# Cross-attention and a mixture of experts on one core: loads to 128 partitions, statistics in one piece, and results fetched earlier

## The chip, the core and the metric

The kernel runs on one core of a Trainium2 chip. The metric is device microseconds for one launch. Three runs of the kernel before gave 607.83, 608.56 and 609.25 us; the median is 608.56. Everything is float32.

## What is computed

```python
def _L0_xattn_ref(query, kv, Wq, Wg, bg, Wkv, Wo):      # 16 heads of 32
    q = query @ Wq.T
    gate = jax.nn.sigmoid(query @ Wg.T + bg)
    k, v = jnp.split(kv @ Wkv.T, 2, axis=-1)
    # heads split; feature map: x + 1 for x > 0, else exp(x)
    kv_summary = jnp.einsum('bhsd,bhse->bhde', k, v)
    k_sum = k.sum(axis=-2)
    z = 1.0 / (jnp.einsum('bhld,bhd->bhl', q, k_sum)[..., None] + EPS)
    attn = jnp.einsum('bhld,bhde->bhle', q, kv_summary) * z
    return attn * gate @ Wo.T                            # heads joined

def _L0_ffn_ref(x, Wr, We, be):                          # 8 experts, 2 a token
    w, sel = jax.lax.top_k(jnp.einsum('bsd,de->bse', x, Wr), 2)
    gate = softmax(w) spread over the chosen experts
    for e in range(8):
        out = out + gate[..., e:e+1] * (x @ We[e] + be[e])

x = x + _L0_xattn_ref(_layernorm(x), ctx_2048, ...)      # x: 4 x 512 x 512, ctx: 4 x 1024 x 512
x = x + _L0_ffn_ref(_layernorm(x), ...)
```

## The kernel before

The kernel goes through the four batches in turn. For each batch there are two parts. `kv_tiles` takes eight tiles of 128 context rows: each one is loaded by SyncE (`load_ctx`, three buffers), multiplied by the key and value halves of wkv (matmuls `pk` and `pv`), the keys go through the feature map (L250 to L252, VectorE and ScalarE), and the sums of keys times values gather in PSUM (`kvs`). Then come the queries (`pq`), the gates (`pg`, sigmoid with bias at L423), the products with the sums (`pz`, `pn`) and the output projection (`po`). The first four context tiles of the next batch are worked off between products and output, the other four behind it, so that TensorE always has something to do.

The layer norm of the attention's input is taken in a layout of its own. `load_blocks` brings x into SBUF in pieces that need only a 32x32 transpose on VectorE (`normalized_T`, L297 and L301). The mean and deviation of each row are computed from an ordinary copy of x (`layernorm_stats`). They must then get to other partitions, and that goes through memory: `spread_moments` writes means and reciprocal deviations to `moments` in two DMAs on GpSimd's queue (L281), waits, and reads them back in four (L286). `load_rows` (wg and wq) and a loop of the same form for the expert weights (L382 and L383) load weights in the matching order of rows, in four DMAs of 32 partitions each, where each partition gets four pieces of 2 KB. For wg the columns are then turned by seven copies on GpSimd (L169). The seven gate biases are loaded by SyncE between the seven pieces of wo (L949 and L950).

After a batch's attention, `choose` normalizes its rows, computes the router's logits, and picks two experts a token. `dispatch` computes a place for every choice and scatters the rows, with GpSimd's indirect DMAs, into `stream`, a region of memory for each expert that has been set empty before (`set_empty`). Then `run` works off tiles of 128 rows of the stream: 17 early ones, mixed in with the fourth batch, and up to 22 late ones, of which 18 (`SURE`) are a fixed loop. For a tile SyncE loads the rows in four DMAs of 32 partitions (L765, tile `xg`, five buffers in all), and the last two columns in a fifth (tile `of`). VectorE transposes (L782), TensorE multiplies by the expert's weights (`pe`), VectorE adds the bias (L814), and GpSimd scatters the results to `result` (L818). In the loop, `rows(j + 5)`, `expert(j)` and `turned(j + 3)` are one step.

The two results of every token are then fetched back (L889), weighed and added to x (L902), and stored (L913), for sixteen tiles of 128 tokens. For the first fourteen this is spread over the steps of the late loop by a table of steps, `begins`: the fetch at that step, the addition three steps later, the store after one more. `queue_of` gives the queue: GpSimd's up to step 12, ScalarE's from step 13 on. A fetch waits for as many puts as `READ` names; whether that was enough is computed in the kernel, and tiles for which it was not are read again at the end. The last two tiles follow after the loop. The work on each engine's queue stands in an order that is mostly fixed in the program (`keep_in_program_order`, `issue_after`); what is left free is placed by the scheduler of the framework.

Of the kernel before, what the change touches and what calls it, by code (L numbers as in the profile page):

```python
# [9 lines left out]
F32 = mybir.dt.float32  # L10
# [7 lines left out]
P = 128  # L18
B, L, S, D = 4, 512, 1024, 512
E, F = 8, 512  # L20
HD = 32
# [32 lines left out]
def xattn_moe_kernel(  # L54
# [32 lines left out]
    result = dram.tile([NOWHERE + 2 * L, F], F32, name="result")  # L87


    moments = dram.tile([B, HD, NT, P // HD, 2], F32, name="moments")  # L90


    def matmul(**operands):
# [8 lines left out]
    def load(dst, src):  # L102
        latest["load"] = nc.sync.dma_start(out=dst, in_=src)  # L103
        tc.keep_in_program_order(latest["load"])
# [27 lines left out]
    def load_rows(dst, w):  # L132


        for i in range(NC):
            load(dst[ts(i, HD)], w.rearrange("(c f) i n -> i f c n", f=HD)[i])

    wkv_sb = wpool.tile([P, NC, 2 * D], F32, tag="wkv", name="wkv_sb")
    wq_sb = wpool.tile([P, NC, D], F32, tag="wq", name="wq_sb")
# [3 lines left out]
    nc.gpsimd.memset(wr_sb, 0.0)  # L143
    bg_sb = wpool.tile([P, NC], F32, name="bg_sb")
    we_sb = wpool.tile([P, E, NC, F], F32, name="we_sb")
    we_rows = we.rearrange("e (c f) i n -> e i f c n", f=HD)

    ctx_tiles = {}

# [104 lines left out]
    def layernorm_stats(tiles):  # L254
        mv = small.tile([P, NT, 2], F32, tag="mv", name="mv")
        for t in range(NT):
            st = small.tile([P, 6], F32, tag="st", name="st")
            nc.vector.bn_stats(st, tiles[t])
            nc.vector.bn_aggr(mv[:, t, :], st)
        rstd = small.tile([P, NT], F32, tag="rstd", name="rstd")  # L260
        nc.scalar.activation(rstd, mv[:, :, 1], AF.Sqrt, bias=eps_sb)
        nc.vector.reciprocal(rstd, rstd)
        return mv, rstd

    def normalize(dst, xt, t, mv, rstd):
        nc.vector.tensor_scalar(
            dst, xt, mv[:, t, 0:1], rstd[:, t : t + 1], ALU.subtract, ALU.mult
        )

    def transposed(dst, src):  # L270

# [4 lines left out]

    def spread_moments(b, tiles):

        mv, rstd = layernorm_stats(tiles)
        for k, of in enumerate((mv[:, :, 0], rstd)):  # L280
            nc.gpsimd.dma_start(  # L281
                out=moments[b, :, :, :, k].rearrange("t n j -> j t n"), in_=of
            )
        ln = small.tile([P, NT, P // HD, 2], F32, tag="ln", name="ln", bufs=1)
        for i in range(NC):
            nc.gpsimd.dma_start(  # L286
                out=ln[ts(i, HD)].rearrange("t n j k -> t (n j k)"),
                in_=moments[b].rearrange("t n j k -> t (n j k)"),
            )
        return ln  # L290

    def normalized_T(xT, t, blocks, ln):

        rows = blocks[:, ts(t, D)].rearrange("p (j f) -> p j f", f=P)
        with tc.issue_after(latest["map"].ins):
            for j in range(P // HD):
                nc.vector.tensor_scalar(  # L297
                    rows[:, j], rows[:, j], ln[:, t, j, 0:1], ln[:, t, j, 1:2],
                    ALU.subtract, ALU.mult,
                )  # L300
            nc.vector.transpose(  # L301
                xT[:, :, ts(t, P)].rearrange("p c (j t) -> p j c t", t=HD),
                rows.rearrange("p j (c f) -> p j c f", f=HD),
            )
# [41 lines left out]
    def kv_blocks(psum):  # L346
        for h in range(P // HD):
            r = slice(h * HD, (h + 1) * HD)
            nc.scalar.copy(h_kv[r], psum[r, :, r])
            nc.vector.tensor_copy(h_ks[r, :, h : h + 1], psum[r, :, P : P + 1])  # L350
# [23 lines left out]
    def kv_tiles(b, lo, hi, between=None, inside=None):  # L374
        for s in range(lo, hi):
            nxt = (b, s + 2) if s + 2 < NS else (b + 1, s + 2 - NS)
            if nxt[0] < B and nxt not in loaded_ctx:
                loaded_ctx.add(nxt)
                ctx_tiles[nxt] = load_ctx(*nxt)
            if b in (1, 2) and s % 2 == 0:  # L380
                e = (b - 1) * E // 2 + s // 2
                for i in range(NC):  # L382
                    load(we_sb[ts(i, HD), e], we_rows[e, i])  # L383
            for e in (s,) if b else (2 * (s - NS // 2), 2 * (s - NS // 2) + 1):
                if e >= 0:
                    set_empty(b, e)
            if s == 0:
                sums[b] = pkv.tile([P, NC, 2 * P], F32, tag="kvs", name="kvs")
            k = made.pop(s) if s in made else keys(b, s)
            if (b, s) == (0, 0):  # L390
                made[1] = keys(0, 1)
            if inside is not None and s == lo:
                inside()
            v = values(b, s)
            if s > 0:
                kv_add(sums[b], s - 1, *pending[b])
            pending[b] = k, v
            if between is not None:
                between(s - lo)
        if hi == NS:  # L400
            kv_add(sums[b], NS - 1, *pending[b])
# [121 lines left out]

    routed = {}

    def choose(b, mv, rstd):

        rows = []
        batch = work.tile([P, NT, ROW], F32, tag="row", name="rows", bufs=1)
        for t in range(NT):  # L530
            row = batch[:, t, :]
            normalize(row[:, 0:D], xs[b][t], t, mv, rstd)
            nc.gpsimd.tensor_copy(row[:, D : D + 1], home[:, b * NT + t : b * NT + t + 1])
            rows.append(row)

        xT = big.tile([P, NC, L], F32, tag="aT", name="x2T")
        for t in range(NT):
            transposed(xT[:, :, ts(t, P)], rows[t])
            yield

        ps = pmm.tile([P, L], F32, tag="mm", name="ps")
        for c in range(NC):
            matmul(
                out=ps[ts(c, HD), :],
                lhsT=wr_sb[:, c, :],
                rhs=xT[:, c, :],
                start=True,
                stop=True,
                tile_position=(0, c * HD),
            )  # L550
        share = work.tile([P, L], F32, tag="z", name="share")
        nc.scalar.copy(share, ps)
        yield
        pl = pmm.tile([P, NT, E], F32, tag="mm", name="pl")
        for t in range(NT):
            matmul(
                out=pl[:, t, :], lhsT=share[:, ts(t, P)], rhs=by_expert, start=True, stop=True
            )
        lg = small.tile([P, NT, E], F32, tag="lg", name="lg")
        nc.vector.tensor_copy(lg, pl)  # L560

        def largest(name):
            m = small.tile([P, NT, 1], F32, tag=f"m{name}", name=f"m{name}")
            hot = small.tile([P, NT, E], F32, tag=f"hot{name}", name=f"hot{name}")
            at = small.tile([P, NT, 1], F32, tag=f"at{name}", name=f"at{name}")
            nc.vector.tensor_reduce(m, lg, AX.X, ALU.max)
            nc.vector.tensor_tensor(hot, lg, m.to_broadcast([P, NT, E]), ALU.is_equal)
            nc.vector.tensor_tensor(hot, hot, rank, ALU.mult)
            nc.vector.tensor_reduce(at, hot, AX.X, ALU.max)
            nc.vector.tensor_tensor(hot, hot, at.to_broadcast([P, NT, E]), ALU.is_equal)  # L570
            return m, hot, at

        m1, hot1, first = largest("1")
        nc.vector.scalar_tensor_tensor(lg, hot1, -BIG, lg, ALU.mult, ALU.add)
        m2, hot2, _ = largest("2")

        routed[b] = rows, m1, hot1, first, m2, hot2
        yield
# [159 lines left out]
    def run(lists, lo, n, early):  # L738
# [3 lines left out]
        def rows(j):  # L742
# [10 lines left out]
            of = small.tile([P, 2], F32, tag="of", name="of", bufs=8)  # L753
            rows_of = stream[ds(row, P), :]
            parts = []
            for i in range(NC):
                parts.append(
                    (
                        xg[ts(i, HD), 0:D].rearrange("t (j f) -> t j f", j=NC),
                        rows_of[:, ts(i, P)].rearrange("(j t) f -> t j f", t=HD),  # L760
                    )
                )
            parts.append((of, rows_of[:, D:ROW]))
# [162 lines left out]
    def plan(step, *what):  # L926
        at_step.setdefault(min(step, SURE), []).append(what)

    def queue_of(step):
        return nc.gpsimd if step < SURE - 5 else nc.scalar  # L930

    begins = (-3, -2, -1, 0, 5, 6, 7, 8, 10, 11, 14, 15, SURE - 2, SURE - 2)
    for g, (lo, hi, most) in enumerate(READ):
        for t in range(lo, hi):
            plan(begins[t], fetch, t, most, queue_of(begins[t]), g)
    for t, begin in enumerate(begins):
        step = begin + (3 if begin < SURE - 4 else SURE)
        plan(step, add, t, gates if step < SURE else gates_end)
        plan(step + 1, store, t, queue_of(step + 1))

    def also(j):
        for what, *of in at_step.pop(j, []):
# [3 lines left out]
    xT = new_xT()  # L946
    kv_tiles(0, 0, 3)
    for g, a, b, n in turned:
        load(bg_sb[b : b + n, g : g + 1], bg[a : a + n, g : g + 1])  # L949
        load(wo_sb[b : b + n, g, :], wo[a : a + n, g, :])  # L950
    ln = spread_moments(0, xs[0])

# [2 lines left out]
            normalized_T(xT, t, blocks, ln)  # L955

    kv_tiles(0, 3, NS, between)
    kv_blocks(sums[0])
    for b in range(B):
        more = b + 1 < B  # L960
# [60 lines left out]
            for _ in range(3):  # L1021
                next(early)
        attention_out(b, aT)
        choice = choose(b, *layernorm_stats(xs[b]))
        if more:

            def between(i):
# [133 lines left out]
```

## Time and profile before

| What | us |
|---|---|
| Median of three runs | 608.56 |
| The profiled execution's own time | 610.59 |
| Span of the profile | 608.9 |
| TensorE busy | 576.7 |
| VectorE busy | 289.6 |
| Loads of late and early rows (xg), 140 issues of | 64 KB |
| Loads of expert weights (we), 32 issues of | 256 KB |

The profile is one execution, and its span is shorter than the execution's own time by 1.7 us that lie around it. A `pk` or `pv` of one tile is eight passes on TensorE (four matmuls, two passes each) and takes 3.43 us without a gap. The chain of work that ended last is followed back from the last instruction, at each step to what released it. "DMA xg<-stream" in it stands for the time between the issue of that transfer and its landing. In tables by stage each row is a stretch of the span.

### The profile page before, as it was taken

The page shows a single profiled execution, that of the slowest core. Times are in us where ns is not written, and L with a number is a line of the kernel's source. Part 1 is how long each engine was busy: PE and PEld are TensorE (multiplying, and loading weights), DVE is VectorE, ACT ScalarE, POOL GpSimd, SP SyncE. Part 2 cuts the span into 40 slices and gives each one's busy share as a digit, 9 for nine tenths or more (in the row PEclk, how much of TensorE's full clock was granted, in tenths as well). Part 3 has the DMA queues.
Part 4 walks back from the last instruction along what each step waited for, and adds up shares of the span by engine and source line. Part 5 has one row for each costly group of instructions (what it writes and reads, how often), then busy time and mean ns, then how long its engine had stood idle before and what let it go on. Part 6 is the DMA issues. An engine that isn't in the chain of part 4 may idle for free.

```text
span 608.9 us, 6440 instructions
## 1 busy us (share of the span) xinstructions
PE 576.7 (95%) x1780; PEld 270.0 (44%) x1780; DVE 289.6 (48%) x732; ACT 109.3 (18%) x168; POOL 120.5 (20%) x289
## 2 busy tenths in 40 slices
PE   7989999999999999999999999999999999998950
PEld 3545544454555435445543454554344443443420
DVE  2215254354317443541564355128765579473863
ACT  1311241220313321122242121221300110000000
POOL 4230021000001510000061100003211237444630
PEclk9989999999999999999999999999999999999995
DMA  8979995374490698627338660952255444889866
GB/s 283 166 122 355 340 197 48 116 238 131 121 277 19 140 240 261 190 87 209 103 140 147 236 203 5 315 221 108 89 119 121 121 122 167 251 235 295 243 225 212
DMA packets 78933, 109.87 MB, mean 180 GB/s; under 512 B 13229, under 2 KB 39853, under 8 KB 78768
## 3 DMA queue, kind: packets, MB, share of 16 engines
q1 hardware_dynamic: 68112, 79.91, 49.0%
q0 software_dynamic: 8336, 24.29, 12.2%
q10 hardware_dynamic: 2448, 5.24, 2.6%
q8 instruction: 15, 0.25, 0.2%
q14 instruction: 22, 0.18, 0.1%
HBM read 50.19 MB, written 59.96 MB: 181 GB/s over the span
## 4 chain that ended last, share of the span: by engine, by line
PE 74%; DMA 9%; DVE 6%; SPq 4%; issue 4%; POOL 1%; DVEq 0%; ACTq 0%; POOLq 0%
PE pk L94 18%; PE pv L94 16%; PE pq L94 9%; PE po L94 9%; PE pg L94 7%; PE pe L94 5%; PE kvs L94 4%; DMA xg<-stream 4%; DMA cT<-in_cT_dram 3%; SPq L765 2%; SPq L103 1%; PE pn L94 1%; PE pt L97 1%; DMA result<-y,to 1%; DMA of<-stream 1%
## 5 line engine op out<-in xcount | busy, mean ns | idle before, releaser
L94 PE MATMUL pk<-wkv_sb,cT 128*128 128x512 f32 x256 | 119.4, 611 | 6.4 <-DMA cT<-in_cT_dram 6.4
L94 PE MATMUL pv<-wkv_sb,cT 128*128 128x512 f32 x256 | 115.2, 593 | 0.0
L250 DVE TENSOR_SCALAR ex<-pk 128x512 f32<-128x512 f32 x32 | 22.1, 692 | 135.1 <-PE pk L94 135.1
L94 PEld LDWEIGHTS pv<-wkv_sb,cT 128*128 128x128 f32 x256 | 48.4, 190 | 62.3 <-issue 59.8
L94 PEld LDWEIGHTS pk<-wkv_sb,cT 128*128 128x128 f32 x256 | 48.0, 196 | 60.9 <-issue 53.4
L94 PE MATMUL pe<-we_sb,xgT 128*128 x144 | 62.8, 594 | 3.9 <-DVE xgT L782 3.9
L94 PE MATMUL pe<-we_sb,turned_rows 128*128 x136 | 60.4, 596 | 1.9 <-DVE turned_rows L782 1.5
L94 PE MATMUL pg<-xT,wg_sb 128*128 128x512 f32 x128 | 56.7, 595 | 0.0
L94 PE MATMUL pq<-xT,wq_sb 128*128 128x512 f32 x128 | 56.6, 596 | 0.0
L94 PE MATMUL po<-wo_sb,aT 128*128 128x512 f32 x128 | 55.6, 592 | 0.0
L818 POOL DMA_INDIRECT result<-y,to x35 | 36.4, 1041 | 94.0 <-DVE y L814 91.3
L251 ACT ACTIVATE ex<-ex 128x512 f32<-128x512 f32 x48 | 30.2, 629 | 137.5 <-DVE ex L250 117.3
L330 POOL MEMSET v<- 128x4 f32 x32 | 3.3, 108 | 245.4 <-PE kvs L94 245.3
L94 PEld LDWEIGHTS pe<-we_sb,xgT 128*128 128x128 f32 x144 | 27.1, 190 | 39.4 <-issue 32.2
L624 POOL DMA_INDIRECT stream<-rows,slot x32 | 32.9, 1027 | 51.7 <-DVE acc L587 22.2
L94 PEld LDWEIGHTS kvs<-v,k 128*128 128x128 f32 x256 | 33.3, 191 | 16.0 <-issue 14.2
L94 PEld LDWEIGHTS pe<-we_sb,turned_rows 128*128 128x128 f32 x136 | 25.2, 190 | 34.0 <-issue 29.9
L94 PEld LDWEIGHTS pg<-xT,wg_sb 128*128 128x128 f32 x128 | 24.0, 190 | 32.1 <-issue 32.1
L94 PEld LDWEIGHTS po<-wo_sb,aT 128*128 128x128 f32 x128 | 24.1, 190 | 29.2 <-issue 28.7
L94 PEld LDWEIGHTS pq<-xT,wq_sb 128*128 128x128 f32 x128 | 23.8, 190 | 27.3 <-issue 27.3
L94 PE MATMUL kvs<-v,k 128*128 128x129 f32 x256 | 34.1, 275 | 0.0
L252 DVE SCALAR_TENSOR_TENSOR k<-pk,ex 128x512 f32<-128x512 f32 x32 | 22.1, 691 | 21.6 <-ACT ex L251 21.6
(183 smaller groups left out, 459.7 us busy)
## 6 DMA issues: line engine op xcount, KB each, us to landing
stream<-empty SPq DMA_DIRECT2D x24, 1028.0 KB
stream<-empty SPq DMA_DIRECT2D x8, 1285.0 KB
xg<-stream SPq DMA_DIRECT2D x140, 64.0 KB
we_sb<-in_we_dram SPq DMA_DIRECT2D x32, 256.0 KB
cT<-in_cT_dram SPq DMA_DIRECT2D x31, 256.0 KB
y<-result POOLq DMA_DIRECT2D x10, 512.0 KB
x<-in_x_dram SPq DMA_DIRECT2D x16, 256.0 KB
blocks<-in_x_dram SPq DMA_DIRECT2D x16, 256.0 KB
```

The costliest lines, as they stand in the source:

```text
L94: tc.keep_in_program_order(nc.tensor.matmul(**operands))
L97: tc.keep_in_program_order(nc.tensor.transpose(dst, src, ident))
L103: latest["load"] = nc.sync.dma_start(out=dst, in_=src)
L250: nc.vector.tensor_scalar(ex, src, 0.0, None, ALU.min)
L251: nc.scalar.activation(ex, ex, AF.Exp)
L252: latest["map"] = nc.vector.scalar_tensor_tensor(dst, src, 0.0, ex, ALU.max, ALU.add)
L330: nc.gpsimd.memset(v[:, :, P : P + 1], 1.0)
L624: put = nc.gpsimd.indirect_dma_start(out=stream, out_offset=bass.IndirectOffsetOnAxis(ap=slots[i][:, t, :], axis=0), in_=rows[t], in_offse ...
L765: load = nc.sync.dma_start(out=dst, in_=src)
L818: put = nc.gpsimd.indirect_dma_start(out=result, out_offset=bass.IndirectOffsetOnAxis(ap=home_i, axis=0), in_=y, in_offset=None, bounds_ch ...
```

## The change

It does four things.

1. The loads of wg, wq, the expert weights and the experts' rows are cut the other way: still four DMAs each, but each now goes to all 128 partitions, with one piece a partition (2 KB for weights, 512 bytes for rows). What was four groups of 32 partitions is now an outermost dimension of 4 on the side of the source. The blocks of x (`load_blocks`) are loaded as before.
2. The reciprocal deviations are written beside the means into `mv`, and one DMA a batch brings both to `moments`, eight numbers (32 bytes) a partition; `normalize` and `normalized_T` read them there. In the order of instructions the writes of the moments come behind the seven copies of wg on GpSimd for the first batch. For the second and third batch's end the next statistics, with ScalarE's square root, stand ahead of the router's copy `share`, where they stood behind it.
3. The seven loads of gate biases leave SyncE's queue for GpSimd's.
4. In `begins`, the tiles 4 to 9 are fetched one step earlier and the tiles 10 and 11 two steps earlier. GpSimd's queue now serves the steps up to 11. The stores of the tiles 8 and 9 go to SyncE's queue, later ones to ScalarE's as before.

```diff
-    moments = dram.tile([B, HD, NT, P // HD, 2], F32, name="moments")
+    moments = dram.tile([B, HD, P // HD, NT, 2], F32, name="moments")
...
-        for i in range(NC):
-            load(dst[ts(i, HD)], w.rearrange("(c f) i n -> i f c n", f=HD)[i])
+        for c in range(NC):
+            load(dst[:, c, :], w[ts(c, HD)].rearrange("f i n -> i f n"))
...
-        rstd = small.tile([P, NT], F32, tag="rstd", name="rstd")
-        nc.scalar.activation(rstd, mv[:, :, 1], AF.Sqrt, bias=eps_sb)
-        nc.vector.reciprocal(rstd, rstd)
-        return mv, rstd
+        dev = small.tile([P, NT], F32, tag="rstd", name="dev")
+        nc.scalar.activation(dev, mv[:, :, 1], AF.Sqrt, bias=eps_sb)
+        nc.vector.reciprocal(mv[:, :, 1], dev)
+        return mv
...
-        mv, rstd = layernorm_stats(tiles)
-        for k, of in enumerate((mv[:, :, 0], rstd)):
-            nc.gpsimd.dma_start(
-                out=moments[b, :, :, :, k].rearrange("t n j -> j t n"), in_=of
-            )
-        ln = small.tile([P, NT, P // HD, 2], F32, tag="ln", name="ln", bufs=1)
+        mv = layernorm_stats(tiles)
+        nc.gpsimd.dma_start(out=moments[b].rearrange("t j n k -> j t (n k)"), in_=mv)
+        ln = small.tile([P, P // HD, NT, 2], F32, tag="ln", name="ln", bufs=1)
...
-                for i in range(NC):
-                    load(we_sb[ts(i, HD), e], we_rows[e, i])
+                load_rows(we_sb[:, e], we[e])
...
-            for i in range(NC):
+            for j in range(P // HD):
                 parts.append(
                     (
-                        xg[ts(i, HD), 0:D].rearrange("t (j f) -> t j f", j=NC),
-                        rows_of[:, ts(i, P)].rearrange("(j t) f -> t j f", t=HD),
+                        xg[:, ts(j, P)],
+                        rows_of[ts(j, HD), 0:D].rearrange("t (i f) -> i t f", i=NC),
                     )
                 )
...
-    def queue_of(step):
-        return nc.gpsimd if step < SURE - 5 else nc.scalar
-
-    begins = (-3, -2, -1, 0, 5, 6, 7, 8, 10, 11, 14, 15, SURE - 2, SURE - 2)
+    def queue_of(step, behind=nc.scalar):
+        return nc.gpsimd if step < SURE - 6 else behind
+
+    begins = (-3, -2, -1, 0, 4, 5, 6, 7, 9, 10, 12, 13, SURE - 2, SURE - 2)
...
-        plan(step + 1, store, t, queue_of(step + 1))
+        plan(step + 1, store, t, queue_of(step + 1, nc.sync if step < SURE - 4 else nc.scalar))
...
-        load(bg_sb[b : b + n, g : g + 1], bg[a : a + n, g : g + 1])
         load(wo_sb[b : b + n, g, :], wo[a : a + n, g, :])
...
     kv_tiles(0, 3, NS, between)
+    for g, a, b, n in turned:
+        nc.gpsimd.dma_start(out=bg_sb[b : b + n, g : g + 1], in_=bg[a : a + n, g : g + 1])
     kv_blocks(sums[0])
```

More of the change, by code (lines that the diff above doesn't have):

```diff
@@ L145, in xattn_moe_kernel @@
     we_sb = wpool.tile([P, E, NC, F], F32, name="we_sb")
-    we_rows = we.rearrange("e (c f) i n -> e i f c n", f=HD)
     ctx_tiles = {}
@@ L259, in layernorm_stats, with normalize @@
             nc.vector.bn_aggr(mv[:, t, :], st)
-        rstd = small.tile([P, NT], F32, tag="rstd", name="rstd")
-        nc.scalar.activation(rstd, mv[:, :, 1], AF.Sqrt, bias=eps_sb)
-        nc.vector.reciprocal(rstd, rstd)
-        return mv, rstd
-    def normalize(dst, xt, t, mv, rstd):
-        nc.vector.tensor_scalar(
-            dst, xt, mv[:, t, 0:1], rstd[:, t : t + 1], ALU.subtract, ALU.mult
-        )
+        dev = small.tile([P, NT], F32, tag="rstd", name="dev")
+        nc.scalar.activation(dev, mv[:, :, 1], AF.Sqrt, bias=eps_sb)
+        nc.vector.reciprocal(mv[:, :, 1], dev)
+        return mv
+    def normalize(dst, xt, mv):
+        nc.vector.tensor_scalar(dst, xt, mv[:, 0:1], mv[:, 1:2], ALU.subtract, ALU.mult)
     def transposed(dst, src):
@@ L277, in spread_moments @@
     def spread_moments(b, tiles):
-        mv, rstd = layernorm_stats(tiles)
-        for k, of in enumerate((mv[:, :, 0], rstd)):
-            nc.gpsimd.dma_start(
-                out=moments[b, :, :, :, k].rearrange("t n j -> j t n"), in_=of
-            )
-        ln = small.tile([P, NT, P // HD, 2], F32, tag="ln", name="ln", bufs=1)
+        mv = layernorm_stats(tiles)
+        nc.gpsimd.dma_start(out=moments[b].rearrange("t j n k -> j t (n k)"), in_=mv)
+        ln = small.tile([P, P // HD, NT, 2], F32, tag="ln", name="ln", bufs=1)
         for i in range(NC):
             nc.gpsimd.dma_start(
-                out=ln[ts(i, HD)].rearrange("t n j k -> t (n j k)"),
-                in_=moments[b].rearrange("t n j k -> t (n j k)"),
+                out=ln[ts(i, HD)].rearrange("t j n k -> t (j n k)"),
+                in_=moments[b].rearrange("t j n k -> t (j n k)"),
             )
@@ L297, in normalized_T @@
                 nc.vector.tensor_scalar(
-                    rows[:, j], rows[:, j], ln[:, t, j, 0:1], ln[:, t, j, 1:2],
+                    rows[:, j], rows[:, j], ln[:, j, t, 0:1], ln[:, j, t, 1:2],
                     ALU.subtract, ALU.mult,
@@ L524, in xattn_moe_kernel, with choose @@
     routed = {}
-    def choose(b, mv, rstd):
+    def choose(b, mv):
         rows = []
@@ L531, in choose @@
             row = batch[:, t, :]
-            normalize(row[:, 0:D], xs[b][t], t, mv, rstd)
+            normalize(row[:, 0:D], xs[b][t], mv[:, t])
             nc.gpsimd.tensor_copy(row[:, D : D + 1], home[:, b * NT + t : b * NT + t + 1])
@@ L1023, in xattn_moe_kernel @@
         attention_out(b, aT)
-        choice = choose(b, *layernorm_stats(xs[b]))
+        choice = choose(b, layernorm_stats(xs[b]))
         if more:
```

## The prediction

> **What bounds the kernel now.** I read the page's busy shares first, then the chain that ended last, then TensorE's own timeline of the last hundred microseconds, then a table of the DMA load by stage.
>
> ```profile
> span 608.9 us, 6440 instructions
> PE 576.7 (95%) x1780; PEld 270.0 (44%) x1780; DVE 289.6 (48%) x732; ACT 109.3 (18%) x168; POOL 120.5 (20%) x289
> ...
> q1 hardware_dynamic: 68112, 79.91, 49.0%
> ```
>
> TensorE is the bound nearly everywhere: 576.7 of 608.9 us. So the change can win only at places where TensorE waits, some 32 us in all, but it can lose without such a limit. The chain shows where those places are: the start and the end.
>
> ```profile
> 26.61 12.30 DMA cT<-in_cT_dram
> 39.05 5.37 PE pk L94 x8
> 44.42 3.43 PE pv L94 x8
> ...
> 590.47 5.94 DMA result<-y,to
> 596.95 5.62 DMA y<-result
> ```
>
> The context tile asked for at 26.61 lands at 38.91; TensorE idles 1.99 us before 39.05, and its next eight matmuls take 5.37 instead of 3.43 us. That stall is worth 2.0 + 1.9 = 3.9 us. The last two lines are the tail: the last result's way to memory and back. Between them, 50 to 440 us, the chain is TensorE without a gap. In the late loop of experts TensorE stands nearly gapless too, at 3.43 us a tile:
>
> ```profile
> 522.53 7.03 PE L94 MATMUL pe<-we_sb,xgT 128*128 x16
> 530.13 31.17 PE L94 MATMUL pe<-we_sb,xgT 128*128 x72 [0.58 <-DVE xgT L782]
> 562.91 20.87 PE L94 MATMUL pe<-we_sb,xgT 128*128 x48 [1.60 <-DVE xgT L782]
> 585.47 3.70 PE L94 MATMUL pe<-we_sb,xgT 128*128 x8 [1.70 <-DVE xgT L782]
> ```
>
> The three gaps (3.9 us) are late rows (xg). Now the DMA load, by stage; the columns are busy time of PE, PEld, DVE, ACT and POOL, then clock, mean busy share of the 16 DMA engines, and GB/s:
>
> ```profile
> 4.00:14.00 10.00, 9.55 (x17) 4.14 (x18) 1.78 (x6) 0.76 (x2) 4.19 (x34) 1.00 1.04 353
> 14.00:24.00 10.00, 10.00 (x31) 4.93 (x30) 4.10 (x11) 3.38 (x5) 3.38 (x3) 1.00 1.04 221
> 24.00:36.00 12.00, 12.00 (x35) 5.79 (x34) 2.77 (x4) 3.13 (x4) 0.00 (x0) 1.00 1.19 105
> 462.00:474.00 12.00, 12.00 (x29) 5.32 (x28) 5.10 (x12) 0.30 (x1) 0.00 (x0) 1.00 0.45 89
> 514.00:532.00 18.00, 15.95 (x38) 6.91 (x38) 9.30 (x19) 0.00 (x0) 8.22 (x18) 1.00 0.80 239
> 532.00:550.00 18.00, 18.00 (x44) 7.95 (x43) 13.23 (x24) 0.00 (x0) 8.83 (x24) 1.00 0.83 238
> 550.00:568.00 18.00, 16.39 (x39) 7.12 (x38) 8.72 (x17) 0.00 (x0) 7.43 (x18) 1.00 0.90 259
> 568.00:590.00 22.00, 19.48 (x45) 8.09 (x43) 14.08 (x26) 0.00 (x0) 10.85 (x24) 1.00 0.78 263
> ```
>
> Loads to 128 partitions (4 to 14 us) move 353 GB/s; the loads of wg and wq, each to 32 partitions (14 to 24), only 221 at the same busy share. From 24 to 36 us, with the 4-byte writes of the moments under way, the full engines move 105. And in the late loop (514 to 590) the engines are already 78 to 90% busy. That is the cover that matters: TensorE is one step ahead of a DMA bound.
>
> **The change, part by part.**
>
> *Wide loads (wg, wq, we, xg).* They seem to answer the second row: 353 instead of 221 GB/s. But the source of each new load is a pattern of 4 x 32 x n, with the 4 outermost, against 128 partitions of destination; before, both sides had 32 outermost. [...] What the trace has: the loads issued by SyncE in the issue table add up to 62720 data packets from 337 issues; the 68112 of queue q1 are 5392 more, which is 337 x 16. So each issue closes with 16 small packets, one for each engine, and all of them have an outermost 32 or more on both sides. No issue of SyncE here has a 4 outermost. [...]
>
> The price. By the first row an engine moves 353/16 = 22 GB/s; the packet records give 84 ns for 2048 bytes, or 24. Four engines: 88 to 98 GB/s, so 1 MB takes 10.7 to 11.9 us.
>
> *Start.* The four engines are free of earlier loads at 14 us (first row's end). Then wg 10.7 to 11.9, one tile 0.7, wq 10.7 to 11.9, the blocks 4.7 (1 MB at 221) and the tile that TensorE waits for 0.7: 41.5 to 43.9, landing 1.5 later: 43 to 45.4 instead of 38.9. **+5** (0 to +8).
>
> *Middle.* The expert weights (we) are 256 KB issues in fours: 10.7 us on four engines per two steps of 7.76 us, beside 2 x 2.8 for emptying the stream and 2 x 0.7 for tiles: 17.7 in 15.5 us. The tiles are asked for two steps (15.5 us) ahead, and the stretch is followed by 13.7 us of attention output, so by itself this hides. If that cover failed, it would cost 2.2 us per pair of steps, in eight pairs. What may not hide: on ScalarE, in the order of instructions, the square root of the next batch's statistics now stands ahead of the copy `share` in two batches. That copy ran at 183.03, with the matmul that needs it at 184.05. Now it waits for x, whose loads queue behind we. Price: from nothing to 4 us each; the statistics of the last x tile, 0.69 + 0.17, and the root, 0.30, alone use the 1.0 us of slack, and x comes some 2 us late. **+4** (0 to +8) for both.
>
> *Experts.* A tile of rows is 512 packets of 512 bytes. The records' median is 27 ns; the row of 462 to 474, where nearly nothing else runs, gives 0.45 x 16 x 12 us for four tiles, 42 ns each, with the 32-partition crowding in it. On four engines: 512 x 27/4 = 3.5 us a tile, up to 5.4. I take 3.5, since crowding should go. Early tiles: the first lands 2.5 us later (3.5 instead of about 1), before TensorE has others to do. **+2.5** (0 to +5). Late loop: 18 tiles x 3.5 = 63 us on these four. Also on them is a sixteenth each of the rest: 514 to 576 moves 239 x 18 + 238 x 18 + 259 x 18 + 263 x 8 = 15.4 MB, less 4.7 MB of rows = 10.7 MB, at 353 to 410 GB/s 26 to 30 us. Together 90 us from the first late request (514.6), so the last rows land at about 607 instead of 578: +29 to +33; **+32** (low +12 if half of the others' work moves behind the rows; at 5.4 us a tile +65).
>
> *Statistics in one piece.* Two writes of 512 4-byte pieces a batch (1.74 and 1.53 us of GpSimd at 18 and 20 us) become one of 128 pieces of 32 bytes. 24 to 36 us moved 1.26 MB that takes 5.7 us at 221 GB/s: some 6 us of DMA time come free. If the four engines were not the late ones, the tile would land before it is needed and the 3.9 us stall would go. With them it is not what ends last: **0** (−3.9 to 0). The new wait of the moments behind the seven copies of wg on GpSimd is covered: ln is needed at 46.5.
>
> *Gate biases.* Seven issues leave SyncE (0.34 to 1.35 us each, 4.3 together, from 27 to 43 us) for GpSimd, idle from 8.6 to 18. The next tile, issued at 43.79, was not waited for: **0** (−1 to 0).
>
> *Results sooner, late stores elsewhere.* Eight fetches of 512 KB come one or two steps earlier; each waits in GpSimd's queue for the put of the step before, with the next put behind it (2 us of cover by five y buffers). Two stores of 0.59 us leave GpSimd for SyncE, whose last row request is by then out. The work of the four engines ahead of the last rows stays the same: **−1** (−4 to +3).
>
> Sum: 5 + 4 + 2.5 + 32 − 1 = +42.5. The profiled execution's own time is 610.59 (span 608.9), the median 608.56, 2 us lower, as the whole; 608.6 + 42 = 650.6, say **650**.
>
> **Rivals.**
> *Sixteen engines.* The hardware cuts the 128 partitions in 16, or takes the four engines in turn. [...] Then the second row becomes the first, the start's 3.9 us and some 3 us of the late gaps go, the tail gains 1: 608.6 − 8 = 601. It decides at about 7 engines: 512 x 27/k + 30/18 stays under 3.43 us a tile from k = 8.
> *Four engines, but mostly hidden.* The rows overtake the results and fetches, which then drain on the twelve idle engines; start and middle keep their cover by the 6 us of freed DMA time. Late +12, elsewhere +3: 624. Against it: the results share those four engines too, and each needs all of its parts.
> *No effect.* Gains and losses cancel; nothing in the rows singles this out.
>
> **Numbers.** Four engines, late loop bound: 0.68 (632 to 682). Mostly hidden: 0.14 (612 to 632). Sixteen engines: 0.16 (596 to 606). No change: 0.02. A measurement of this kernel tells about 0.2% from nothing. The range 612 to 682 leaves out the sixteen-engine case and little else. Slower 0.82, same 0.02, faster 0.16.
>
> **What would show it.** Right: q1 has fewer packets by 12 for each new load (180 of them); 14 to 36 us below 221 GB/s; the first big wait for a tile ends after 42; in the late loop TensorE waits for xg on most tiles at 5 to 6 us each, DMA share near half. Wrong: the packets stay 16 an issue and 14 to 24 us moves over 300 GB/s; or the loop keeps 3.5 us a tile.

## The result and the profile after

The changed kernel takes 674.36 us (median of four runs, 672.74 to 678.69), the kernel before in the same session 608.9 us (607.83 to 609.35). The ratio is 1.109, with a 95% interval of 1.1035 to 1.1143: slower by 65 us. The profiled execution took 674.17 us, its span is 672.5.

First the page's busy shares and the line of SyncE's DMA queue (packets, MB, share of the engines):

```profile
span 672.5 us, 6434 instructions
PE 595.0 (88%) x1780; PEld 275.7 (41%) x1780; DVE 291.9 (43%) x732; ACT 108.9 (16%) x168; POOL 113.2 (17%) x292
...
q1 hardware_dynamic: 65616, 80.42, 37.9%
```

Two things are to be seen. TensorE is busy for 18.3 us more, with the same 1780 matmuls. And q1 has 2496 packets fewer. That number comes out exactly: the seven bias loads that left take 624 with them (512 of data and 7 x 16 that close them), two stores of 256 KB that came in bring 288, and 180 loads that close with 4 packets instead of 16 lose 180 x 12 = 2160. 68112 − 624 + 288 − 2160 = 65616. That is what is left if every one of the changed loads ran on four engines. The packets that close a load have 4 bytes in the packet records: q1 has 5904 of that size before, 512 of them biases, and 3152 after. The packets under way agree: from 14 to 24 us the kernel before has 16 or 17 packets of 2 KB under way for 71% of the time; from 26 to 35 us the kernel after has four of them for 78% and five for 20%, and never more than six. All four loads of wq had been asked for by 25.52, so they share these four; which of the sixteen engines they are, the records don't name.

The table by stage of the kernel after (busy time of PE, PEld, DVE, ACT and POOL, then clock, DMA share, GB/s):

```profile
14.00:24.00 10.00, 10.00 (x30) 4.88 (x29) 3.85 (x11) 3.38 (x5) 0.00 (x0) 1.00 0.33 113
24.00:36.00 12.00, 12.00 (x37) 5.89 (x36) 2.77 (x4) 3.13 (x4) 3.80 (x10) 1.00 0.43 118
36.00:46.00 10.00, 0.81 (x8) 0.61 (x6) 0.00 (x0) 0.59 (x1) 1.81 (x5) 0.66 0.83 152
...
590.00:620.00 30.00, 21.45 (x44) 8.42 (x43) 12.04 (x23) 0.00 (x0) 10.55 (x29) 0.89 0.59 189
```

From 14 to 36 us a share of 0.33 to 0.43 of the DMA engines is busy, though SyncE has a full list of loads to give out: 113 and 118 GB/s. From 36 to 46 us TensorE does next to nothing. In the late loop the DMA share is 0.59 where it was 0.78 to 0.90, and TensorE works 21.45 of 30 us, at a clock of 0.89.

TensorE's own timeline of the kernel after shows three of the four places where the time went (start, length; in brackets the idle time before and what ended it). They are the start, the middle (one of two such waits) and the late loop:

```profile
48.54 5.84 PE L94 MATMUL pk<-wkv_sb,cT 128*128 128x512 f32 x8 [11.73 <-DMA cT<-in_cT_dram]
54.22 3.60 PE L94 MATMUL pv<-wkv_sb,cT 128*128 128x512 f32 x8
...
198.62 1.87 PE L94 MATMUL pl<-by_expert,share 128*128 128x8 f32 x8 [4.68 <-ACT share L545]
...
563.49 8.83 PE L94 MATMUL pe<-we_sb,xgT 128*128 x16 [2.58 <-DVE xgT L775]
...
578.50 3.70 PE L94 MATMUL pe<-we_sb,xgT 128*128 x8 [1.46 <-DVE xgT L775]
...
605.68 8.91 PE L94 MATMUL pe<-we_sb,xgT 128*128 x16 [5.62 <-DVE xgT L775]
...
632.60 12.54 PE L94 MATMUL pe<-we_sb,xgT 128*128 x24 [5.80 <-DVE xgT L775]
```

The second column matters as much as the brackets. Before, eight passes take 3.60 to 3.70 us from the first start to the last end, and 16 take 7.03. Sixteen passes behind a gap of 2.58 or 5.62 us take 8.8 to 8.9 us; eight passes behind a gap of 1.46 us take the usual 3.70. So these two gaps cost their own length and some 1.8 us more, and the one of 1.46 us its length alone.

The ledger, by positions in the two timelines:

| Stage | Mark in the timeline, before and after | Longer by, us | Predicted |
|---|---|---|---|
| Start | `pv` of the context tile that is waited for, 44.26 and 54.22 | 10.0 | 5 |
| Middle | first `pq` of the last batch, 409.66 and 435.64 | 16.0 | 4 |
| Early experts | first late `pe`, 522.53 and 557.21 | 8.7 | 2.5 |
| Late loop | end of the last `pe`, 589.17 and 651.32 | 27.5 | 32 |
| Tail | end of the span, 608.9 and 672.5 | 1.4 | −1 |

### The profile page after: what moved, and what is told of

Its sections match the earlier page's. It is cut to its first block, busy times and chain, and to the rows that moved or that the text cites. A ratio compares the mean times of both kernels' runs of the same rounds, so it can differ in the third digit from the quotient of the medians.

```text
span 672.5 us, 6434 instructions
## 1 busy us (share of the span) xinstructions
PE 595.0 (88%) x1780; PEld 275.7 (41%) x1780; DVE 291.9 (43%) x732; ACT 108.9 (16%) x168; POOL 113.2 (17%) x292
## 3 DMA queue, kind: packets, MB, share of 16 engines
q10 hardware_dynamic: 2160, 4.72, 2.2%
## 5 line engine op out<-in xcount | busy, mean ns | idle before, releaser
L94 PE MATMUL pe<-we_sb,xgT 128*128 x144 | 71.0, 644 | 23.1 <-DVE xgT L775 22.9
L94 PE MATMUL pe<-we_sb,turned_rows 128*128 x136 | 63.9, 623 | 7.1 <-DVE aT L465 3.9
L94 PE MATMUL pq<-xT,wq_sb 128*128 128x512 f32 x128 | 60.7, 631 | 0.0
L94 PEld LDWEIGHTS pq<-xT,wq_sb 128*128 128x128 f32 x128 | 25.5, 204 | 29.8 <-issue 29.5
L775 DVE STREAM_TRANSPOSE xgT<-xg 128x512 f32<-128x512 f32 x18 | 12.8, 712 | 53.9 <-DMA xg<-stream 53.9
```

The costliest lines, as they stand in the source:

```text
L94: tc.keep_in_program_order(nc.tensor.matmul(**operands))
L775: latest["turn"] = nc.vector.transpose(xT.rearrange("p c (j t) -> p j c t", t=HD), xg[:, 0:D].rearrange("p (j c f) -> p j c f", j=NC, f=HD),)
```

## The experiments

My theory: the wide loads run on four engines, and are the whole loss, by three separate ways (rows, expert weights, wg and wq). The rivals: one of the other parts loses too (the square root ahead of `share`, SyncE's longer issues, the earlier fetches), or 128 partitions are bad in themselves.

### All loads back in their old form (e1)

From the kernel after:

```diff
-        for c in range(NC):
-            load(dst[:, c, :], w[ts(c, HD)].rearrange("f i n -> i f n"))
+        for i in range(NC):
+            load(dst[ts(i, HD)], w.rearrange("(c f) i n -> i f c n", f=HD)[i])
...
-                        xg[:, ts(j, P)],
-                        rows_of[ts(j, HD), 0:D].rearrange("t (i f) -> i t f", i=NC),
+                        xg[ts(i, HD), 0:D].rearrange("t (j f) -> t j f", j=NC),
+                        rows_of[:, ts(i, P)].rearrange("(j t) f -> t j f", t=HD),
```

> The changed kernel with only its loads put back: wg, wq, the expert weights and the experts' rows again go to 32 partitions with 32 outermost on both sides; the statistics in one piece, the gate biases, the earlier fetches and the stores stay changed. Theory (the loads with a 4 outermost run on four engines and cost all of it): about 603 us, 600 to 608, a little faster than before, since the first big wait for a context tile (2.0 us before 39.05, and 1.9 in slow matmuls after it) goes with the moments' small writes. Rival (ScalarE's square root ahead of the copy share, and fetches that wait in GpSimd's queue, cost much by themselves): 620 us or more, with TensorE waiting for share for several us.

Measured: 605.2 us, ratio 0.994 (0.9911 to 0.9969). The loss is gone, and what is left of the change gains 3.2 us on the 608.41 of that session. The wait for the context tile at 39 us is not there any more. And the square root is behind `share` again, though nothing was done to it: it was not the new statistics that moved it.

### Each group of wide loads alone

From the kernel before, with one group of loads in the new form each: the rows (e2), the expert weights (e3), wg and wq (e4).

```diff
 e2   +                        xg[:, ts(j, P)],
      +                        rows_of[ts(j, HD), 0:D].rearrange("t (i f) -> i t f", i=NC),
 e3   +                    load(we_sb[:, e, c, :], we[e][ts(c, HD)].rearrange("f i n -> i f n"))
 e4   +            load(dst[:, c, :], w[ts(c, HD)].rearrange("f i n -> i f n"))
```

> The kernel before with only the experts' rows (xg) loaded to 128 partitions. Theory (four engines): nothing changes up to the early tiles at 437 us; from there to the last expert matmul the span grows as it did in the changed kernel, 8.5 us in the early stage and 27 in the late loop: about 608.6 + 36 = 645 us, 635 to 655. Rival (the loop became slow through the earlier fetches and the queues, not the rows): within 5 us of before.

> The kernel before with only the expert weights (we) loaded to 128 partitions. In the kernel before the next statistics stand behind the copy share on ScalarE. Theory A (the 16 us of the middle come from we on four engines AND the order on ScalarE, both needed): about no change, 607 to 612 us. Theory B (we on four engines alone holds up x or context tiles): 620 us or more.

> The kernel before with only wg and wq loaded to 128 partitions. Theory (four engines, and SyncE held up behind them, so that the context tile is asked for late): the start grows by as much as in the changed kernel, 10 us, or somewhat more since the moments' small writes are still there: 616 to 624 us. Rival (the start grew because of the moments' new place behind the copies of wg on GpSimd, or the gate biases): within 3 us of before.

| Kernel | Median, us | Ratio (95%) | Packets of q1, fewer by |
|---|---|---|---|
| rows wide | 639.71 | 1.0528 (1.0486 to 1.0569) | 1680 = 140 x 12 |
| expert weights wide | 626.23 | 1.0294 (1.0249 to 1.0338) | 384 = 32 x 12 |
| wg and wq wide | 621.39 | 1.0225 (1.0186 to 1.0263) | 96 = 8 x 12 |

All three lose: 31.3, 17.8 and 13.0 us. With −3.2 for the rest they add up to 58.9 of the 65.5 us; the other 6.6 us appear only with all of them together. The traces say where: by the marks of the ledger the early experts take 4.8 us more with wide rows alone and 8.7 with the whole change, the late loop 24.5 and 27.5. Why they do was not tried. The packet counts say four engines for each group by itself. The waits of TensorE in the version with wide expert weights (in total, times, longest) tell where its loss is:

```profile
PE pl L94 <- ACT share L552: 9.7, 2, 4.9
```

Not at the experts, which find their weights in time, but at the router, twice. Slow matmuls come on top: TensorE is busy for 583.7 us instead of 576.7. The time is the one that theory B expected; e5 will tell the two apart. Nothing but the form of the loads of we differs from the kernel before, and yet the scheduler has put the square root ahead of `share` here too.

### The order on ScalarE, with the expert weights still wide (e5)

To the version with wide expert weights I added one constraint: the statistics of the next batch come behind a late step of the router.

```diff
-        mv, rstd = layernorm_stats(tiles)
+        with tc.issue_after(latest["picked"].ins) if "picked" in latest else nullcontext():
+            mv, rstd = layernorm_stats(tiles)
```

> The kernel before with the expert weights loaded to 128 partitions (as in the run that took 626 us), and with the next batch's statistics held behind the router's last step, so that VectorE's and ScalarE's order is again that of the kernel before. Theory (the middle's loss needs both: x some us late behind we on four engines, and the square root ahead of the copy share): 607 to 612 us, no wait of TensorE for share. Rival (we on four engines costs by itself, through context tiles or x): 618 us or more.

Measured: 608.25 us, ratio 1.0016 (0.999 to 1.0043), against 1.0294 without the constraint. The count of packets is that of four engines still (67728), and the loads cost nothing. ScalarE's timeline of this version:

```profile
181.97 0.58 ACT L553 COPY share<-ps 128x512 f32<-128x512 f32 x1 [1.26 <-PE ps L94]
```

The copy is released by TensorE's `ps`, as it should be. In the kernel after it stood behind the root, which waits for x:

```profile
191.68 1.28 ACT L260 ACT_TABLE_LOAD   x1
197.80 0.30 ACT L260 ACTIVATE dev<-mv,eps_sb 128x4 f32<-128x4 f32 x1 [4.83 <-DVE mv L258]
198.00 0.57 ACT L545 COPY share<-ps 128x512 f32<-128x512 f32 x1
```

ScalarE idles 4.83 us for the statistics, with `share` next in its queue and TensorE behind that.

### Weights to 128 partitions, on sixteen engines (e6)

From the version with the old loads: wg, wq and we lie in memory in the order of the partitions, so that each of their loads goes to 128 partitions with 128 outermost on both sides. Only the layout of the weights in memory differs, and it is made ahead of the launch.

```diff
-        for i in range(NC):
-            load(dst[ts(i, HD)], w.rearrange("(c f) i n -> i f c n", f=HD)[i])
+        for c in range(NC):
+            load(dst[:, c, :], w[c])
...
```

> The kernel that took 605.2 us (rows to 32 partitions, all else as changed), but wg, wq and the expert weights go to 128 partitions from arrays that lie in memory in the order of the partitions, so that both sides have 128 outermost. The computation is the same; only the layout in memory of the weights differs. Theory (four engines did the harm, 128 partitions are good): loads of weights run at 350 GB/s or more where the 32-partition loads ran at 221; start as in the 605 us run or better; the square root may stand ahead of share again, with x in time: 602 to 608 us. Rival (loads to 128 partitions with pieces of 2 KB are slow in themselves, or the order on ScalarE alone costs): 615 us or more.

Measured: 605.88 us, ratio 0.9966 (0.9946 to 0.9986). TensorE's waits and one row by stage:

```profile
PE pl L94 <- ACT share L545: 0.5, 2, 0.3
```

```profile
14.00:24.00 10.00, 10.00 (x31) 4.94 (x30) 3.65 (x11) 3.38 (x5) 3.49 (x9) 1.00 0.86 242
```

The same 128 partitions, with the other dimension outermost, move 242 GB/s and not 113, and q1 has the 67776 packets of the version with the old loads, none fewer. So it isn't the number of partitions. The 242 GB/s are less than the 350 that were expected; the engines' share in that row is 0.86, so they were not full; but from 18 to 24 us, at 1.01, they moved no more than 257. And the root stands ahead of `share` in this version too; x is on time, and it costs 0.5 us instead of 9.8. The loss in the middle needs both, the order and a late x. The higher rate for the weights brings nothing beyond what the old loads give with the same statistics (605.2 us).

### Rows wide, on two queues (e7)

In the kernel after, four issues for a tile hold SyncE for 2.89 us (0.72 each), where they held it 1.85 (0.46 each). To see whether that sets the pace of the late loop, I took the version with wide rows alone, and two of the four loads of each late tile go out from ScalarE (the main lines of the edit):

```diff
+                queue = nc.scalar if not early and part in (1, 3) else nc.sync
+                load = queue.dma_start(out=dst, in_=src)
```

> The kernel before with the experts' rows loaded to 128 partitions (639.7 us), and of each late tile's four loads two issued on ScalarE's queue, which is idle there. In the changed kernel four such issues held SyncE 2.9 us where they held it 1.85, about 4.6 us a tile with the rest. Theory A (the four engines are the bound of the late loop, 3.5 us of rows and 1.5 to 2 of other packets a tile): same within 4 us, 636 to 643. Theory B (SyncE's issuing is the bound): 15 us or more faster, 625 or less.

Measured: 637.43 us, ratio 1.0478 (1.0439 to 1.0517), beside 1.0528 (1.0486 to 1.0569) on one queue. TensorE's waits:

```profile
PE pe L94 <- DVE xgT L783: 20.4, 15, 3.1
```

The waits are more and shorter (15 with a longest of 3.1 us; on one queue 13, longest 6.0, 23.2 us in total). The loss stays, so SyncE's issuing is not the bound. That the four engines are it can be estimated from the packet records of the kernel after. From 560 to 640 us the packets of rows keep 2.87 engines busy on average, and all packets together 9.22. With the rows on four engines and the rest spread evenly over sixteen, each of the four is busy for 0.72 + 0.40 = 1.1 of the time, as much as in the full stage from 14 to 24 us before (1.04).

### The rest of the change, part by part

From the version with the old loads, the steps of fetches and stores were put back as well (e8, which leaves statistics and biases). From the kernel before, the statistics alone (e9) and the biases alone (e10) were changed. The edits are the hunks of the change itself.

> The kernel that took 605.2 us with the steps of the fetches and the queues of fetches and stores put back too; what is left of the change is the statistics in one piece and the gate biases. Theory (the gain of 3 us is the start's stall of 3.9 us, lifted by the one-piece statistics; the steps give at most 1): 604 to 607 us, in the profile no wait for a context tile at 39 us. Rival (the gain comes from fetching sooner): 608 us or more.

> The kernel before with the statistics in one piece a partition and nothing else. My theory: the write of the many 4-byte pieces is what slowed every load between 24 and 36 us, so without it the context tile of the 3.9 us wait at 39 us lands in time and the kernel takes 603 to 606 us, the whole gain of the version with the old loads. The rival (the biases on GpSimd's queue made that gain, by leaving SyncE's queue seven transfers shorter) expects 607 to 609 us here and the wait still there.

> The kernel before with the gate biases on GpSimd's queue and nothing else. My theory expects 607 to 610 us, no change that can be told, with a wait for a context tile near 39 us as before. The rival expects 603 to 606 us and no wait there.

| Kernel | Median, us | Ratio (95%) |
|---|---|---|
| statistics, biases, steps (e1) | 605.2 | 0.994 (0.9911 to 0.9969) |
| statistics, biases (e8) | 603.28 | 0.9929 (0.9905 to 0.9954) |
| statistics (e9) | 604.17 | 0.9922 (0.9895 to 0.9949) |
| biases (e10) | 608.54 | 0.9995 (0.9963 to 1.0027) |

The one-piece statistics make the whole gain, 3 to 6 us; the intervals of the first three overlap, so steps and biases give nothing that can be told. These three beat both kernels. The stage from 24 to 36 us shows why, first with the statistics alone, then with the biases alone:

```profile
24.00:36.00 12.00, 12.00 (x35) 5.84 (x34) 2.77 (x4) 3.13 (x4) 4.71 (x12) 1.00 1.02 187
```

```profile
24.00:36.00 12.00, 12.00 (x35) 5.83 (x34) 2.77 (x4) 3.13 (x4) 1.81 (x4) 1.00 1.15 110
```

At full engines 187 GB/s move instead of 105; the other loads are no longer held up by the 4-byte writes. With the statistics alone TensorE has no wait for a context tile left but the very first of the kernel. With the biases alone the wait near 39 us was there in the profiled execution, but shorter, 0.62 us and not 1.99. One profiled execution proves little beside a median that doesn't move.

## Why the prediction was right, and where it was off

**The mechanism was right.** The sizes were less so. The total is 24 us above the 650 and inside the range, but three of the stages (start, middle, early experts) cost more than their own ranges allow. That the new loads run on four engines, on which the forecast is built, was the author's assumption, taken against the reading that sixteen would take part: nothing in the profile of before shows it, since no issue of SyncE there has a 4 outermost. The packet counts bear it out load by load, 12 fewer for each, in the kernel after and in each of e2, e3 and e4, and e6 shows the other side: with 128 outermost no packet is missing (67776, as with the old loads).

**Late loop, +32, measured +27.5.** The step was 18 tiles at 3.5 us on four engines and a sixteenth of everything else, at up to 410 GB/s (4096 bytes in 159 ns, the median of GpSimd's packets of that size before, on sixteen engines). The rows' own term held: their packets took 28 ns on average, so 512 of them on four engines are 3.6 us a tile (an estimate). The loop took 651.3 − 557.2 = 94 us, 5.2 a tile, with a DMA share of 0.57 to 0.60, as expected. That the sum came so near is in part luck. It was to be 90 us from the first late request, so that the last rows land at about 607 instead of 578. But 514.6 + 90 is 604.6, and 578 is not when the last rows had landed before. VectorE's last lines for rows, before and after, show it:

```profile
584.71 0.71 DVE L782 STREAM_TRANSPOSE xgT<-xg 128x512 f32<-128x512 f32 x1 [2.23 <-DMA xg<-stream]
```

```profile
646.86 0.71 DVE L775 STREAM_TRANSPOSE xgT<-xg 128x512 f32<-128x512 f32 x1 [4.62 <-DMA xg<-stream]
```

With 584.7, the step as priced gives some +20 to +22. The stretch from the first late request (514.60 and 549.29) to these lines took 97.6 us instead of 70.1: 7.6 us more than the 90, and 27.5 more than before. The two slips worked against each other. On TensorE's side the same 27 us are 22.9 us of waiting for rows instead of 3.9 (+19.0), and 71.0 instead of 62.8 us for its 144 matmuls of these tiles (+8.2). With rows as the bound, part of these 8.2 us would have been waiting otherwise; that was not taken apart. Moving half of the issues to another queue (e7) did not free the loop.

**Start, +5 (0 to +8), measured +10.0.** Up to wq the step held: wg was there at 26.0, as 14 + 10.7 to 11.9 says, and the DMA share rises from 0.43 (24 to 36 us) to 0.83 (36 to 46) about where wq was to end (36.1 to 38.5). The term that failed is what follows. The blocks and the tile were counted at 221 GB/s and the tile at 0.7 us; from 36 to 46 us the engines, at a share of 0.83, moved 152. The 1.5 us to the tile's landing were an estimate; the shortest way from issue to landing that the chain of before has for rows, at 438.48, is 1.85 us. SyncE's timeline of the kernel after adds how the tile came to be asked for so late:

```profile
17.38 8.14 SPq L103 DMA_DIRECT2D wq_sb<-in_wq_dram  x4
25.56 11.43 SPq L103 DMA_DIRECT2D blocks<-in_x_dram  x4
...
40.72 0.38 SPq L103 DMA_DIRECT2D cT<-in_cT_dram  x1
```

The second column is the time that SyncE was held by the issues: 8.14 us for four (1.85 before) and 11.43 (4.15 before). What held SyncE that long was not shown. With it the tile was asked for at 40.72 and not at 26.61, and could not use the engines that a share of 0.33 to 0.43 left idle up to 36 us.

**Middle, +4 (0 to +8), measured +16.0.** The place was named (the root ahead of `share`, twice, with x behind we), the price was not. The step took the last x tile's statistics and 2 us of lateness, "nothing to 4 us each". Measured: two waits of 4.7 and 5.1 us, 9.8 together. VectorE's timeline of the kernel after shows why:

```profile
194.81 1.33 DVE L257 BATCH_NORM_STATS2 st<-x 128x6 f32<-128x512 f32 x2 [5.10 <-DMA x<-in_x_dram]
...
196.28 1.27 DVE L257 BATCH_NORM_STATS2 st<-x 128x6 f32<-128x512 f32 x2
```

VectorE waits 5.10 us for the first x tile, and then the statistics of all four run one after another without a wait (2.6 us), so the four tiles landed as good as together and not one by one. The lateness itself was as priced: x is there at 194.81, 1.9 us behind the 192.92 at which `share` was due (1.13 us behind the start of `ps`, as before). What was mis-sized is the statistics, 2.6 us for four tiles in place of 0.86 for one, and the slow matmuls, which were left out. The matmuls `pq` take 60.7 instead of 56.6 us, `pl` 5.7 instead of 3.8: 9.8 + 4.1 + 1.9 = 15.8 of the 16.0. One statement ahead of the prediction does not hold either: the order on ScalarE was taken for a part of the change to the statistics. e1 and e3 show that it follows from the form of the loads of we, by way of the scheduler.

**Early experts, +2.5 (0 to +5), measured +8.7.** Here waits of TensorE came that were hardly there before: 3.9 us for `aT` (0.4 before), 3.2 for early rows (1.5), and `pe` on early rows takes 63.9 instead of 60.4 us: 3.5 + 1.7 + 3.5 = 8.7. Why `aT` is late can be read from VectorE's timeline, before and after:

```profile
440.41 0.71 DVE L782 STREAM_TRANSPOSE turned_rows<-xg 128x512 f32<-128x512 f32 x1 [2.81 <-DMA xg<-stream]
```

```profile
469.87 0.71 DVE L775 STREAM_TRANSPOSE turned_rows<-xg 128x512 f32<-128x512 f32 x1 [5.63 <-DMA xg<-stream]
470.50 0.23 DVE L782 TENSOR_SCALAR to<-of,rankedA 128x1 uint32<-128x1 f32 x1
470.65 1.28 DVE L465 TENSOR_TENSOR aT<-pz,aT 128x512 f32<-128x512 f32 x2
```

The transpose of the first early tile stands ahead of `aT` on VectorE and waits for the rows. They were asked for at 436.86 and 463.88, so they came after 3.6 and 6.0 us: 2.4 us later, just as priced. What the step left out is the work on VectorE that stands behind them, a wait of 3.0 us for a later one of these tiles (1.5 before), and the slow matmuls. The version with wide rows alone has the same wait for `aT` (3.2 us).

**The missed term: TensorE's slow matmuls behind a gap.** The prediction charged them at the start alone, where its row showed them (5.37 us; 3.60 is usual). The same price came in later stages too, behind gaps of 2.58 to 5.80 us. The rows around the gap of 2.58 us in the kernel after show what it is (the last three numbers are clock, DMA share and GB/s):

```profile
560.91:564.92 4.01, 1.43 (x4) 0.72 (x5) 1.47 (x3) 0.00 (x0) 0.46 (x1) 1.00 0.54 179
564.92:568.33 3.41, 3.41 (x6) 1.32 (x5) 1.00 (x3) 0.00 (x0) 1.24 (x4) 0.50 0.71 224
```

The gap ends at 563.49, and 1.4 us later the granted clock is halved for 3.41 us. The trace's record of the clock has eight such stretches ahead of the last matmul, each 3.41 us long or two, three or four times that; the kernel before has one. TensorE is busy for 33.7 us of the eight and for 3.4 us of the one, and at half the clock half of that is lost: some 15 us more than before (an estimate). In all TensorE is busy for 595.0 − 576.7 = 18.3 us more, of the 63.6 by which the span grew. By the ledger the sum of 42.5 is 21.1 us short of 63.6: start, middle and early experts were taken 23.2 us too low, the tail 2.4, and the late loop 4.5 too high.

**Statistics, 0 here and −3.9 without the four engines:** e9 gives −4.5 us (608.65 to 604.17). In the kernel after the wait for the tile is there all the same, but the start is 10.0 us later, and 12.2 with wg and wq alone wide (e4), so some 2 us may have been gained; that is one profile of each. **Biases, 0:** so it was (e10). **Fetches and stores, −1 (−4 to +3):** nothing that can be told (e1 beside e8).

**The rivals.** "Mostly hidden" failed in the late loop, since the rows themselves were most of the work of the four engines (0.72 of 1.1, by the estimate at e7). "Sixteen engines" was worth less than its 601 us even for a load that has them: e6 gives the weights sixteen and ends at 605.88, since the start's 3.9 us were already had from the statistics. For the rows sixteen engines with 128 partitions were not tried.

## What to carry to other kernels

Before cutting a load the other way, look at the outermost dimension on both sides, and count the queue's packets after: a count that fell by 12 a load went with four engines here. The number of partitions was not the point here; four outermost lost 65 us where 32 had lost nothing. And when a wait is priced, price its second half too: the matmuls behind it, and on an engine with a fixed order whatever stands behind the instruction that waits.

## What the runs showed of the hardware that was not expected

- A gap on TensorE slowed what followed, but not by its length alone. In these timelines gaps up to 1.70 us (before, e7) left the next eight passes at 3.70 us, and gaps of 2.58 us and more (after) cost 1.5 us or more. Between them it went both ways: 5.37 us behind 1.86 (e2), 1.93 (e3) and 1.99 (before) and 5.40 behind 2.20 (e7), but 3.70 behind 2.49 (after). In the clock records of before and after, ahead of the last matmul, the granted clock fell to 0.50 for 3.41 us, or for two, three or four times that, and was 1.00 again behind it. Why the same length of gap cost time in one place and not in another was not shown.
- With four outermost, an issue of SyncE for rows took 0.72 us (after) instead of 0.46 (before), even at 464 us, with the DMA share at 0.24 (450 to 480 us). For expert weights four issues took 2.31 us at the shortest, and 1.85 in most cases before.
- Two writes of 512 pieces of 4 bytes held the rest of the loads to 105 to 114 GB/s for 12 us (24 to 36 us of before, e2 and e7), at a DMA share of 1.19 to 1.30. One write of 128 pieces of 32 bytes let 187 to 212 through (e9, e6, e1), at 1.02 to 1.15.
- Before, loads to 32 partitions took a median of 160 ns for a packet of 2 KB between 14 and 24 us, loads to 128 partitions 84 between 4 and 14. After, the loads on four engines took 87 between 14 and 24 us. So in that stage packets at 160 ns, 16 or 17 at a time, moved 221 GB/s, and packets at 87 ns, mostly four at a time, 113.
